# A hybrid of convolution and attention on one core: when pieces of other work are issued between the exponentials

## The chip, the cores and the metric

The kernel runs on one core of a Trainium2 chip. The metric is device time in microseconds (us) of one launch; the shown time is the median of three runs. A profile is one more execution, recorded by the hardware profiler, with its own time.

The engines that matter: TensorE (PE in the profile; PEld is its weight loads) multiplies, ScalarE (ACT) computes exp and tanh, VectorE (DVE) and GpSimd (POOL) do elementwise work, SyncE (SP) issues most DMAs. Each takes its instructions in the order of the program.

## The reference

The input x is 4 images of 64 x 64 pixels with 128 channels, float32. Two layers follow.

```python
# layer 0, per image of N = 4096 pixels
c1 = conv3x3(elu(x), W1) + b1
a, b = split(conv3x3(c1, W2) + b2)
c3 = a * sigmoid(b)
q, k, v = c3 @ Wq + bq, c3 @ Wk + bk, c3 @ Wv + bv      # 4, 4 and 16 wide
probs = softmax of q k^T / 4 over earlier pixels only
x = x + c3 + tile(probs @ v, 8) @ W3 + b3

# layer 1, on t = x as 4096 tokens
y = layernorm(t)
attn = 16 heads of width 8, full softmax(q k^T), no scale
h = y + attn @ wo
t = t + h + (silu(h @ w1) * (h @ w3)) @ w2              # 344 hidden
y = layernorm(t)
t = t + top-2 of 8 experts of y, weighted by the router's softmax
```

What costs most is layer 1's attention: 4 images x 16 heads x 4096 x 4096 exponentials.

## The kernel before

The function `fast_path` writes out every engine's order by hand: the class `InOrder` ties each instruction of an engine to the one before it. (A second function, `general_path`, serves inputs whose scores are out of range and isn't entered here.)

**Turns.** After a start in which the first image's first queries and keys are made, one loop at the end of `fast_path` runs the rest, a turn at a time. A turn is one step of attention: 128 keys of 4 heads against 512 queries. Four score matmuls write two of three PSUM buffers s, each 128 x 1024; two activations exp turn them into e in SBUF; later, value matmuls add e times the values into the one PSUM bank acc. The value matmuls of a step can be issued in quarters of 128 queries, and stay up to 8 quarters behind the scores (`undone`, `behind`, `must`). 32 steps make a segment: one group of 4 heads, one block of 512 queries. At its end VectorE copies acc to at, which is stored. There are 4 groups, 8 blocks and 4 images; the first image's segments are cut into parts, since its keys come one by one. 144 more steps are those of layer 0's attention (`first_step`).

**Pieces.** All other work is cut into pieces by generators: convolutions by a Winograd scheme (`convolutions`, `winograd`), layer 0's projections (`first_attention`), layer 1's operands (`second_operands`), and for each block of queries what follows attention (`last_part`: wo, the gated product, layer norm, router, experts). A piece is mostly a product into the one PSUM bank m, and a VectorE instruction that reads m. Its generator yields the TensorE time that it took and a word: "held" means that the bank holds half a product, "stop" that the next piece may come when there is room, "free" that the next turn shall begin with it.

**The planner.** The kernel is planned when it is built. `turn_at` is the planned start of the turn, 1.81 us apart. `dve_time` and `pool_time` keep clocks of VectorE and GpSimd, `dve_at` and `pool_at`; `bank_at` is when VectorE will have read m last. In each turn, after the scores, `left` is TensorE's planned room:

```python
    EXPS, SCORES, VALUES, PIECE, HEAD, AHEAD = 1.81, 0.54, 0.218, 0.446, 0.23, 0.2
...
        left = ahead + EXPS - SCORES - VALUES * must
        took, beside = None, False
        if not quiet[0] and fillers and fillers[0][3] and not waiting:
            took = insert()
...
        empty = bank_held[0] or bank_at[0] <= turn_at[0] + 0.3 or batches[b].second < NQ
```

A "free" piece comes first, whatever is left. Then the jobs of VectorE's tile (below), then up to two pieces, if the bank is empty, `credit` is above 0, and there is room (or `credit` is above 1.5). Then values take what is left, as long as more than 6 quarters are behind. Up to 0.2 us of unused room (`AHEAD`) is carried to the next turn. `credit` grows each turn by a rate that spreads the remaining pieces over the remaining steps, up to 3.0.

**VectorE's tile.** Of the 32 steps of a whole segment, step 20's exponentials are computed by VectorE instead of ScalarE, by a polynomial (the class `Beside`). The scores come in four units, one head each, through the bank m; each unit has a VectorE instruction that reads m into ey and eight more, queued in `beside_todo`. `beside_work(until)` issues these while VectorE's clock would finish them by `until`, which is the turn's planned start plus 2.9 us. When all four are made (`ready == NSLOT` and `done_at` no later than 0.4 us into the turn), two half products add them to acc. They read ey and write acc, not m. A job's `age` counts turns; its halves are due at 22 and 24. What isn't done at the segment's last values is forced then (`beside_rest`). There are 112 such tiles.

Of the kernel before, what the change touches and what calls it, by code (L numbers as in the profile page):

```python
# [21 lines left out]
NQ = N // QB  # L22
# [104 lines left out]
def fast_path(ctx: ExitStack, tc: tile.TileContext, a: dict, where: dict, out: bass.AP, verdict):  # L127
# [6 lines left out]
    nc = tc.nc  # L134
    x = a["x"]
    B = x.shape[0]
    pe, act, sp = (InOrder(tc, e) for e in (nc.tensor, nc.scalar, nc.sync))

    turn_at, dve_at, pool_at, bank_at = [0.0], [0.0], [0.0], [0.0]

    def pool_time(name, args):

        aps = [x for x in args if hasattr(x, "shape")]
        if aps and name != "dma_start":
            took = 0.65 + 1.25e-3 * int(np.prod(aps[0].shape[1:]))
            pool_at[0] = max(pool_at[0], turn_at[0] + 0.5) + took

    power_at, before, shift = [0.0], [None], [0.0]

    def dve_time(name, args):  # L150

        aps = [x for x in args if hasattr(x, "shape")]

        def reads(prefix):
            return any(x.name.startswith(prefix) for x in aps[1:])

        from_bank = reads("m_") or any(x.name == "m" for x in aps[1:])
        in_sbuf = not any(x.space == bass.MemoryType.PSUM for x in aps)
        took = max(int(np.prod(x.shape[1:])) for x in aps[:2]) / 960.0
        if in_sbuf and name in ("tensor_scalar", "tensor_copy"):  # L160
            took *= 0.5
        took += 0.075
        if any(x.name == before[0] for x in aps[1:]):
            took += 0.117
        before[0] = aps[0].name
        begins = 0.0
        if from_bank:
            begins = turn_at[0] + 1.1 + shift[0]
        elif reads("acc"):
            begins = turn_at[0] + 1.85  # L170
        elif reads("e_"):
            begins = turn_at[0] + 2.2
        elif reads("rs_") and name == "tensor_scalar":
            begins = power_at[0] + 1.3
        begins = max(dve_at[0], begins)
        if in_sbuf and begins < pool_at[0] - 0.2:
            took += 0.75
        dve_at[0] = begins + took
        if aps[0].name.startswith("ve_"):
            power_at[0] = dve_at[0]  # L180
        if from_bank:
            bank_at[0] = dve_at[0]

    dve, pool = InOrder(tc, nc.vector, dve_time), InOrder(tc, nc.gpsimd, pool_time)

    const = ctx.enter_context(tc.tile_pool(name="f_const", bufs=1))
    big = ctx.enter_context(tc.tile_pool(name="f_big", bufs=1))
# [254 lines left out]
    def winograd(u, cols, v, bias, used, final):  # L442

        late = []
        for q, j in enumerate(COLS):
            sd = chunk("sd")
            s, d = wk.tile([P, QB // 2], FP, tag="sums", bufs=1, name="sums"), sd[:, : QB // 2]
            for pair in ((1, 2), (0, 3)):
                if late:
                    late.pop(0)()  # L450
                ps = bank()
                part = [ps[:, : QB // 2], ps[:, QB // 2 :]]
                for m, i in zip(part, pair):
                    product(m, u[:, 4 * i + j, cols], v[q][:, i])
                    if i == pair[0]:
                        yield 0.46, "held"
                if pair[0] == 1:
                    if alone[0]:
                        act.activation(sd, ps, AF.Copy)
                    else:  # L460
                        dve.tensor_copy(sd, ps)
                    dve.tensor_tensor(s, d, sd[:, QB // 2 :], ALU.add)
                    dve.tensor_tensor(d, d, sd[:, QB // 2 :], ALU.subtract)
                else:
                    t = chunk("neg", "t2")
                    if q == 0:

                        dve.scalar_tensor_tensor(t[:, : QB // 2], part[0], bias, s, ALU.add, ALU.add)
                        dve.scalar_tensor_tensor(t[:, QB // 2 :], d, bias, part[1], ALU.add, ALU.subtract)
                    else:  # L470
                        dve.tensor_tensor(t[:, : QB // 2], part[0], s, ALU.add)
                        dve.tensor_tensor(t[:, QB // 2 :], d, part[1], ALU.subtract)
                    used(q)
                    if q == 0:
                        one = t
                    elif q == 1:
                        both, less = chunk("pos", "both"), chunk("pos", "less")
                        (dve if alone[0] else pool).tensor_tensor(both, one, t, ALU.add)
                        pool.tensor_tensor(less, one, t, ALU.subtract)
                    elif q == 2:  # L480
                        late += final(0, t, both, ALU.add)
                    else:
                        late += final(1, less, t, ALU.subtract)
                yield 0.46, "free" if q == 3 and pair[0] == 0 and late else "stop"
        while late:
            late.pop(0)()
            yield 0.0, "free" if late else "stop"
# [53 lines left out]
    def convolutions(b, st):  # L541
# [4 lines left out]
        def elu(n):  # L546
# [4 lines left out]
            for at in range(len(todo) + 2 if todo else 0):  # L551
# [10 lines left out]
                    act.activation(neg[a_], xs[a_], AF.Exp)  # L562
                if c_ is not None:
                    r, k = divmod(c_, 2)
                    ps = bank()
                    transposed(pos[c_], ps)
                    put = [(r, slice(1 + 8 * k, 9 + 8 * k), slice(0, 8))]
                    if k == 0 and r > 0:
                        put.append((r - 1, slice(17, 18), slice(0, 1)))
                    if k == 1 and r < 3:  # L570
                        put.append((r + 1, slice(0, 1), slice(7, 8)))
                    for band, to, of in put:
                        dve.tensor_scalar(
                            e_band[band % 2][:, to, 1 : IMG + 1], rows(ps)[:, of], -1.0, None, ALU.add
                        )
# [102 lines left out]
    def first_attention(b, st):  # L678
# [3 lines left out]
        for c in range(NQ):  # L682
# [10 lines left out]
            if c + 1 < NQ:  # L693
                xt = load_x(b, c + 1, "xt")

            ps = bank()
            yield from halves(ps, wq0, c3)
            u, qx0 = chunk("u"), chunk("qx0")
# [55 lines left out]
    def second_operands(b, st):  # L754
# [7 lines left out]
        cols = slice(c * QB, (c + 1) * QB)  # L762


        for pair in range(2):
            ps = bank()[:, : 2 * (C + 1)].rearrange("p (k c) -> p k c", k=2)
            for i in range(2):
                k = 2 * pair + i
                product(ps[:, i, :], at[:, k * P : (k + 1) * P], w3f)
            rs = small("rs0", [2])  # L770
            dve.tensor_scalar(rs, ps[:, :, C], 1e-35, None, ALU.add)
            dve.reciprocal(rs, rs)
            for i in range(2):
                tk = by_k(t)[:, 2 * pair + i, :]
                dve.scalar_tensor_tensor(tk, ps[:, i, :C], rs[:, i : i + 1], tk, ALU.mult, ALU.add)
            if pair == 1:
                st.read += 1
            yield 0.46, "free" if pair == 1 else "stop"
# [9 lines left out]
        yield from turned_over(h, yT, d["h"][c], "qx0", b == 0)  # L788
        def terms(i, w):

            ps = bank()
            yield from halves(ps, w, yT)
            u = chunk("u")
# [309 lines left out]
    def last_part(b, c):  # L1103
        d = scratch[b]
        while fetch(b, c):
            yield 0.0, "free"
        t, h, an = fetched.pop((b, c))
        ps = bank()
        tokens(ps, an, wo1, range(2))
        yield 0.46, "held"  # L1110
        tokens(ps, an, wo1, range(2, 4))
        dve.tensor_tensor(h, ps, h, ALU.add)
        yield 0.46, "stop"
        ps = bank()
        transposed(h, ps)
        hT = chunk("pos", "hT")
# [2 lines left out]
        yield 0.6, "stop"  # L1119
        gT = [chunk("u", "g0T"), chunk("qx0", "g1T"), chunk("w", "g2T")]  # L1120
        for n, (lo, size) in enumerate(FCH):
            ps = bank()
            yield from halves(ps, fw1[:, lo : lo + size], hT, size)
            h1, th = chunk("neg", "h1"), chunk("sd", "th")
# [5 lines left out]
            dve.scalar_tensor_tensor(h1[:size], ps[:size], 0.5, h1[:size], ALU.mult, ALU.mult)  # L1130
            dve.scalar_tensor_tensor(gT[n][:size], th[:size], 1.0, h1[:size], ALU.add, ALU.mult)
            yield 0.46, "stop"
        ps = bank()
        for m in range(4 * len(FCH)):
            k, n = divmod(m, len(FCH))
# [18 lines left out]
        if not alone[0]:  # L1154
            sp.dma_start(out=d["y"][c], in_=y)
        yield from turned_over(y, yT, d["y"][c], "neg", alone[0])
        ps = bank()
        few_by_token(ps[:, :P], rw, yT)
        scores = sm.tile([P, 4, SLOT], FP, tag="few", name="scores")
# [329 lines left out]
    credit, waiting = 0.0, False  # L1489


    EXPS, SCORES, VALUES, PIECE, HEAD, AHEAD = 1.81, 0.54, 0.218, 0.446, 0.23, 0.2
    ahead = 0.0
    while True:
        turn_at[0] += EXPS
# [22 lines left out]
            rate = (sum(part[1] for part in fillers) + later) / max(40, sum(steps_left) - 160)  # L1518
        credit = min(3.0, credit + rate)
        must = max(0, behind() - 8)  # L1520
        left = ahead + EXPS - SCORES - VALUES * must
        took, beside = None, False
        if not quiet[0] and fillers and fillers[0][3] and not waiting:
            took = insert()
# [2 lines left out]
        empty = bank_held[0] or bank_at[0] <= turn_at[0] + 0.3 or batches[b].second < NQ  # L1527
        for job in jobs:
            cost = HEAD if job.units < NSLOT else PIECE
            if job.can() and empty and (left >= cost or job.late()):  # L1530
                if not (quiet[0] or bank_held[0] or steps_in or waiting):
                    job.piece()
                    left -= cost
                    beside = True
# [17 lines left out]
        ahead = min(max(left, 0.0), AHEAD)  # L1552
        for job in jobs:
            job.step()
        beside_work(turn_at[0] + 2.9, any(job.age > 3 * job.units + 4 for job in jobs if job.halves < 2))
    finish(0)
    alone[0] = True
    run_alone([(r for part in fillers for r in part[0])], lambda: False)
# [717 lines left out]
```

## Time and profile before

| | us |
|---|---|
| median of 3 runs (2 others: 7976.11, 7983.8) | 7978.71 |
| the profiled execution | 7979.66 |
| its span, from the first to the last instruction | 7977.8 |
| TensorE busy (matmuls) | 7760.0 |
| ScalarE busy | 7661.9 |
| VectorE busy | 4798.3 |
| GpSimd busy | 671.5 |
| exponentials e, 8256 of them: busy | 7600.4 |

The clock granted to TensorE was 0.992 of full speed on average. All instructions bear the line of the helper that issues them (line 114), so groups are told apart by their tiles: s, e, acc, m and so on. A group's line gives its count, its busy time and the mean of one, and the engine's idle time just before it with what ended most of that time. A line of the view of waits says who waited for whom, the sum, how many times, and the longest. A matmul's recorded duration holds its passage through the array, while the next one runs already; so the sum of gaps between records is less than the time in which TensorE had nothing to issue. From 74.6 us to 7909.6 us after the start exponentials run; before it is the first image's start, after it the last block's `last_part`.

### The profile page before, as it was taken

What the parts mean: (1) busy time and instruction counts of PE and PEld (TensorE: products, weight loads), DVE (VectorE), ACT (ScalarE), POOL (GpSimd) and SP (SyncE); (2) the same over time, 40 slices, a digit from 0 to 9 for tenths busy, and PEclk for the clock granted to TensorE, in tenths of its full rate; (3) what the DMA queues carried; (4) which work ended last, traced back from release to release, by engine and by line L of the source; (5) the groups of instructions that cost most, each with busy time, mean ns of one, the idle gap of its engine ahead of it and who ended that gap; (6) DMA issues with size and microseconds to landing.
All of it is one profiled execution on the core that took longest, in us unless ns stands there. A gap on an engine that the chain in (4) does not pass through costs nothing.

```text
span 7977.8 us, 237947 instructions
## 1 busy us (share of the span) xinstructions
PE 7760.0 (97%) x103701; PEld 3280.2 (41%) x103701; DVE 4798.3 (60%) x9289; ACT 7661.9 (96%) x8459; POOL 671.5 (8%) x592
## 2 busy tenths in 40 slices
PE   7899999999999999999999999999999999999998
PEld 3333444444444444444444444444444333333334
DVE  4333556462666776666666776666666666666664
ACT  1899999999999999999999999999999999999996
POOL 1201211000022100000001210000000000000000
PEclk9999999999999999999999999999999999999998
DMA  2222011111110111111010011111111111111221
GB/s 71 70 68 69 23 60 33 60 41 53 35 34 15 50 39 50 38 31 43 25 41 29 19 43 43 51 42 34 33 29 52 50 49 53 50 54 50 70 73 38
DMA packets 334834, 360.96 MB, mean 45 GB/s; under 512 B 148211, under 2 KB 224467, under 8 KB 333779
## 3 DMA queue, kind: packets, MB, share of 16 engines
q1 hardware_dynamic: 329763, 343.87, 13.6%
q8 instruction: 814, 13.34, 0.7%
q10 hardware_dynamic: 4016, 1.77, 0.1%
q14 instruction: 241, 1.97, 0.1%
HBM read 209.50 MB, written 136.05 MB: 43 GB/s over the span
## 4 chain that ended last, share of the span: by engine, by line
PE 44%; issue 2%; DVE 2%; ACT 2%; DMA 0%; POOL 0%; SPq 0%; ACTq 0%; DVEq 0%; POOLq 0%
PE acc L114 22%; PE s L114 13%; PE m L114 9%; ACT e L114 1%; DVE ey L114 1%; DVE h L114 0%; DVE em L114 0%; DVE t L114 0%; DVE eg L114 0%; DVE by_e L114 0%; DMA blocks<-d_y 0%; SPq L114 0%; POOL rs L114 0%; DVE f_c_band L114 0%; DVE c L114 0%
## 5 line engine op out<-in xcount | busy, mean ns | idle before, releaser
L114 ACT ACTIVATE e<-s 128x1024 f32<-128x1024 f32 x8256 | 7600.4, 1113 | 111.2 <-PE s L114 106.6
L114 PE MATMUL acc<-e,vg 128*9 128x128 f32 (+3 forms) x61880 | 4278.8, 387 | 1.9 <-DVE at L114 1.8
L114 PE MATMUL s<-qx,f_kx 32*128 32x512 f32 (+1 forms) x16512 | 2556.8, 495 | 88.7 <-ACT e L114 56.4
L114 PEld LDWEIGHTS acc<-e,vg 128*9 128x9 f32 x61880 | 1562.0, 90 | 1777.6 <-issue 1209.5
L114 PEld LDWEIGHTS s<-qx,f_kx 32*128 32x128 f32 (+1 forms) x16512 | 1049.1, 182 | 2068.4 <-ACT e L114 1337.7
L114 DVE SCALAR_TENSOR_TENSOR ey<-ey,eg 128x512 f32<-128x512 f32 x1344 | 940.2, 700 | 31.9
L114 DVE COPY at<-acc 128x512 f32<-128x512 f32 x131 | 90.6, 691 | 597.9 <-PE acc L114 593.4
L114 PE MATMUL m<-v,f_wino 128*32 128x256 f32 x5376 | 420.2, 391 | 12.0 <-POOL v L114 7.3
L114 DVE TENSOR_SCALAR ey<-m 128x512 f32<-128x512 f32 x448 | 307.6, 687 | 89.8 <-PE m L114 80.0
L114 DVE SCALAR_TENSOR_TENSOR eg<-em,ey 128x512 f32<-128x512 f32 x448 | 316.7, 707 | 11.4
L114 DVE SCALAR_TENSOR_TENSOR ey<-ey,em 128x512 f32<-128x512 f32 x448 | 316.7, 707 | 9.5
L114 POOL TENSOR_TENSOR rs<-ve,f_minus_half 128x4 f32<-128x4 f32 x64 | 65.3, 1020 | 3027.4 <-DVE ve L114 2995.0
L114 DVE SCALAR_TENSOR_TENSOR ey<-eg 128x512 f32<-128x512 f32 x448 | 312.7, 698 | 0.0
L114 POOL TENSOR_TENSOR v<-r 128x1024 f32<-128x1024 f32 x112 | 219.1, 1962 | 975.4 <-PE m L114 975.0
L114 DVE COPY sd<-m 128x512 f32<-128x512 f32 x168 | 116.0, 690 | 301.5 <-PE m L114 301.1
L114 PE MATMUL m<-f_we,y2T 128*32 128x256 f32 x3968 | 291.9, 388 | 0.0
L114 DVE TENSOR_TENSOR by_e<-m,gates 128x512 f32<-128x512 f32 x248 | 170.3, 687 | 176.7 <-PE m L114 175.5
L114 PE MATMUL m<-hT,f_fw 128*32 128x256 f32 (+1 forms) x2728 | 233.0, 390 | 1.3 <-DVE hT L114 1.2
L114 POOL TENSOR_TENSOR t<-t,h 128x512 f32<-128x512 f32 x32 | 44.5, 1391 | 2240.6 <-DVE h L114 2240.6
L114 DVE TENSOR_TENSOR t<-m,t 128x512 f32<-128x512 f32 x61 | 42.2, 692 | 308.9 <-PE m L114 308.8
L114 DVE TENSOR_SCALAR em<-ey 128x512 f32<-128x512 f32 x448 | 200.4, 447 | 13.7
L114 DVE TENSOR_SCALAR em<-em 128x512 int32<-128x512 int32 x448 | 196.1, 438 | 10.0
(260 smaller groups left out, 4381.3 us busy)
## 6 DMA issues: line engine op xcount, KB each, us to landing
f_kx<-d_k SPq DMA_DIRECT2D x139, 512.0 KB
qx<-d_q SPq DMA_DIRECT2D x152, 256.0 KB
d_q<-two SPq DMA_DIRECT2D x64, 512.0 KB
d_a<-at SPq DMA_DIRECT2D x128, 256.0 KB
vg<-d_v SPq DMA_DIRECT2D x32, 576.0 KB
d_k<-two SPq DMA_DIRECT2D x32, 512.0 KB
d_v<-vc SPq DMA_DIRECT2D x32, 288.0 KB
xe<-in_x_dram SPq DMA_DIRECT2D x32, 256.0 KB
```

What stands on the lines that cost most here:

```text
L114: made = op(*args, **kw)
```

## The change

It has five parts, all in `fast_path`.

1. `ready_at` notes, for each tile that VectorE or GpSimd writes, the time on their build-time clocks at which it is made. `until_made(*tiles)` yields "free" without issuing anything as long as one of the tiles is made later than 0.4 us into the turn. It stands ahead of the products of v (Winograd), pos (transposes of elu), c3 (wq0), at (w3f), yT (wq1, wk1, router), an (wo1), h (transposes), hT (fw1) and the three gT (fw2). It does nothing in the start, or while the first image's operands aren't all made.
2. `act_time` counts activations that don't read PSUM, 0.16 us and 0.7 ns per element of a row (0.52 us for 512): tanh and the exponentials of xe. `left` of the next turn is larger by their sum.
3. `SCORES` is 0.55 for 0.54 and `PIECE` 0.456 for 0.446.
4. The half products of VectorE's tile are issued without the tests of the bank and of layer 0's steps, and don't keep other pieces out of the turn.
5. From a job's age of 19 on, with its halves not done, `beside_work` may issue VectorE's instructions up to 0.7 us further ahead per turn of age.

```diff
+    ready_at, act_more = {}, [0.0]
+
+    def act_time(name, args):
+
+        aps = [x for x in args if hasattr(x, "shape")]
+        if aps and name == "activation" and aps[1].space != bass.MemoryType.PSUM:
+            act_more[0] += 0.16 + 0.7e-3 * int(np.prod(aps[0].shape[1:]))
...
             pool_at[0] = max(pool_at[0], turn_at[0] + 0.5) + took
+            ready_at[aps[0].name] = pool_at[0]
...
         dve_at[0] = begins + took
+        ready_at[aps[0].name] = dve_at[0]
...
+    act = InOrder(tc, nc.scalar, act_time)
+
+    def until_made(*tiles):
+
+        while not alone[0] and batches[0].second == NQ and max(ready_at.get(x.name, 0.0) for x in tiles) > turn_at[0] + 0.4:
+            yield 0.0, "free"
...
+                yield from until_made(v[q])
                 ps = bank()
...
+            yield from until_made(c3)
             ps = bank()
             yield from halves(ps, wq0, c3)
...
-    EXPS, SCORES, VALUES, PIECE, HEAD, AHEAD = 1.81, 0.54, 0.218, 0.446, 0.23, 0.2
+    EXPS, SCORES, VALUES, PIECE, HEAD, AHEAD = 1.81, 0.55, 0.218, 0.456, 0.23, 0.2
...
-        left = ahead + EXPS - SCORES - VALUES * must
+        left = ahead + EXPS + act_more[0] - SCORES - VALUES * must
+        act_more[0] = 0.0
...
-            if job.can() and empty and (left >= cost or job.late()):
-                if not (quiet[0] or bank_held[0] or steps_in or waiting):
+            if job.can() and not (quiet[0] or waiting) and (left >= cost or job.late()):
+                if job.units == NSLOT:
+                    job.piece()
+                    left -= cost
+                elif empty and not (bank_held[0] or steps_in):
                     job.piece()
                     left -= cost
                     beside = True
...
-        beside_work(turn_at[0] + 2.9, any(job.age > 3 * job.units + 4 for job in jobs if job.halves < 2))
+        hurry = max([0.7 * (job.age - 18) for job in jobs if job.units == NSLOT and job.halves < 2] + [0.0])
+        beside_work(turn_at[0] + 2.9 + hurry, any(job.age > 3 * job.units + 4 for job in jobs if job.halves < 2))
```

The other eight calls of `until_made` stand in the same way ahead of their products.

More of the change, by code (lines that the diff above doesn't have):

```diff
@@ L136, in fast_path @@
     B = x.shape[0]
-    pe, act, sp = (InOrder(tc, e) for e in (nc.tensor, nc.scalar, nc.sync))
+    pe, sp = InOrder(tc, nc.tensor), InOrder(tc, nc.sync)
     turn_at, dve_at, pool_at, bank_at = [0.0], [0.0], [0.0], [0.0]
+    ready_at, act_more = {}, [0.0]
[3 more added lines that the diff above has]
+            act_more[0] += 0.16 + 0.7e-3 * int(np.prod(aps[0].shape[1:]))
     def pool_time(name, args):
@@ L564, in elu @@
                     r, k = divmod(c_, 2)
+                    yield from until_made(pos[c_])
                     ps = bank()
@@ L762, in second_operands @@
         cols = slice(c * QB, (c + 1) * QB)
+        yield from until_made(at)
         for pair in range(2):
@@ L789, in terms @@
         def terms(i, w):
+            yield from until_made(yT)
             ps = bank()
@@ L1107, in last_part @@
         t, h, an = fetched.pop((b, c))
+        yield from until_made(an)
         ps = bank()
@@ L1113, in last_part @@
         yield 0.46, "stop"
+        yield from until_made(h)
         ps = bank()
@@ L1121, in last_part @@
         for n, (lo, size) in enumerate(FCH):
+            yield from until_made(hT)
             ps = bank()
@@ L1132, in last_part @@
             yield 0.46, "stop"
+        yield from until_made(*gT)
         ps = bank()
@@ L1156, in last_part @@
         yield from turned_over(y, yT, d["y"][c], "neg", alone[0])
+        yield from until_made(yT)
         ps = bank()
```

## The prediction

> **What bounds the kernel now.** I read the page from the top, then the windows view of 400 to 7910 us (after the start, before the end), then who waited for whom in that stretch, then timelines of single waits.
>
> ```profile
> PE 7760.0 (97%) x103701; PEld 3280.2 (41%) x103701; DVE 4798.3 (60%) x9289; ACT 7661.9 (96%) x8459; POOL 671.5 (8%) x592
> PE   7899999999999999999999999999999999999998
> ACT  1899999999999999999999999999999999999996
> ...
> L114 ACT ACTIVATE e<-s 128x1024 f32<-128x1024 f32 x8256 | 7600.4, 1113 | 111.2 <-PE s L114 106.6 <-ACT e L114 0.6
> ...
> 400.00:7910.00 7510.00, 7401.23 (x101076) 3125.31 (x101072) 4613.33 (x8873) 7453.62 (x8225) 588.54 (x490) 1.00 0.14 44
> ```
>
> ScalarE and TensorE are both above 95% in every slice but the ends, so the one that sets the pace has to be found by waits.
>
> ```profile
> engine line waited for: us in total, times, longest us
> PEld s L114 <- ACT e L114: 1271.7, 2258, 1.7
> ...
> ACT e L114 <- PE s L114: 51.8, 45, 9.8
> ...
> PE s L114 <- ACT e L114: 54.2, 161, 1.0
> PE acc L114 <- DVE ey L114: 11.4, 10, 2.1
> PE s L114 <- DMA f_kx<-d_k: 10.2, 1, 10.2
> PE m L114 <- DVE f_e_band L114: 4.9, 3, 2.4
> PE m L114 <- DVE sd L114: 4.2, 6, 1.6
> PE m L114 <- DVE yT L114: 4.1, 6, 2.9
> PE m L114 <- DVE y2T L114: 2.4, 2, 1.5
> ```
>
> The reader is to see that the weight load of the scores s waits for ScalarE's e 2258 times, more than half of 4018 turns. That wait doesn't show as idle TensorE, because the matmul before it is still draining. **ScalarE is the bound.** Its exponentials start 904 ns apart when nothing is missing (4714 of the 8074 pairs of neighbours lie within 8 ns of that). I went through all their starts between 400 and 7905 us. 8037 of them at 0.904 us make 7265 us; the stretch has 235 us more. 83 us of it are tanh and exp of pieces (ScalarE takes 0.52 us more for a tanh), some 24 us are small change, and **128 us are turns in which ScalarE started 0.1 us after the scores ended, so TensorE was late**. These I sorted by what TensorE did in the turn. In 103 turns it stood still over 0.1 us for an input (63.3 us of ScalarE's time). In 1224 turns nothing was missing, and the turn was filled too full, by 53 ns each (65.1 us). TensorE itself waits 518 us inside the four score matmuls for the buffer, 0.13 us a turn. So it has room on the average, and what can be won is how its work is spread. That room can't be saved up: three score buffers let it be no further ahead, though the planner carries up to 0.2 us over.
>
> **The change, part by part, in ScalarE's time.**
>
> *Pieces put off (until_made).* Of the 63.3 us, waits for inputs at the places now guarded: yT 6.7, f_e_band or pos 6.2, y2T 2.2, c3 1.6, hT 1.5. To these comes at, which 22 of 24 products found made less than 0.1 us before (2.8 us in full turns). The clocks know only what stands before a tile on its engine. At 2668 us yT stood behind seven ey and em instructions, which they do know. At 2311 us VectorE itself waited 1.47 us for ScalarE's neg, and at 7805 us 2.5 us for blocks from a DMA, which they don't. So yT, c3, hT and at are in reach, 12.6 us; pos and y2T are not. Against it: a piece that comes back is taken at the turn's start without the tests of bank and room. The nearest row is the eb product, two pieces forced into one turn, late by 0.155 us 43 times; 60 pieces put off would cost 9 us so. The products themselves stay as many. I take **-8**, ends -13 and +9. While the first image's operands aren't done, until_made does nothing, so the 10.2 us for f_kx at 754 us stay.
>
> *VectorE's tile: halves without the bank test, and handed over early.* 448 units and 224 half products stay as they are. Waits for ey cost ScalarE 19.5 us in 10 places, and turns that hold a half and are too full 5.7 us. One such place:
>
> ```profile
> 1394.83 0.68 DVE L114 SCALAR_TENSOR_TENSOR ey<-eg 128x512 f32<-128x512 f32 x1
> 1395.54 2.14 DVE L114 SCALAR_TENSOR_TENSOR ey<-ey,eg 128x512 f32<-128x512 f32 x3
> 1395.76 0.11 PEld L114 LDWEIGHTS acc<-ey,vg 128*9 128x9 f32 x6 [0.24 <-issue]
> 1395.76 0.61 PE L114 MATMUL acc<-ey,vg 128*9 128x256 f32 x6
> 1397.72 0.69 DVE L114 SCALAR_TENSOR_TENSOR ey<-ey,em 128x512 f32<-128x512 f32 x1
> 1398.47 0.09 PEld L114 LDWEIGHTS acc<-ey,vg 128*9 128x9 f32 x1 [2.59 <-DVE ey L114]
> ```
>
> The half started at 1395.76 while the last ey ended at 1398.41: the build-time clock held the tile for made 2.7 us too soon, 13 turns before the segment's end. That error stays. What goes is the crowding at the end, where a half held back by the bank meets the last values. I take the 5.7 us and a quarter of the 19.5: **-10**, ends -25 and the rival below. Handing over earlier sets ey work ahead of the bank's readers on VectorE: at age 24 by 0.7 x 6 = 4.2 us, six instructions of 0.69 us. Behind these stand the copy out of m and, at a segment's end, at from acc; the next piece and the next segment's values wait for them. Now TensorE waits 4.2 us for sd and 2.1 us for ey out of m, 6.3 together. I take that two thirds of as much again come: **+4**, ends 0 and 60 (a wait of 0.54 us for each of the 112 tiles, half of the 2.9 - 1.81 = 1.09 us by which the work handed over reaches beyond a turn already).
>
> The Trainium skill speaks against this edit (PSUM — Partial Sum Buffer, section Engine vs sequencer instructions): VectorE's queue is a strict FIFO. By that rule alone, one reader of m caught behind each of the 112 tiles would cost up to 112 x 4.2 = 470 us, an estimate; the row at 2668 us shows one such wait, of 2.90 us. I stay with the small sum, since the planner puts no new piece on a bank whose reader its clock has late.
>
> *Lead counts tanh.* 93 tanh, 28 gate tanh and 26 exp of xe in the stretch take ScalarE 0.52 us each, 76 us in which TensorE now only waits (the tanh's followers: its weight loads waited 52.5 us for th). The turn after gets room for one piece more. Usable room grows from 518 - 76 = 442 to 518 us, by 17%; 17% of the 65.1 us are 11. I take **-10**, ends 0 and -30.
>
> *SCORES and PIECE 0.01 higher.* A turn with a piece is planned 0.02 us fuller than now, so one quarter of values (0.218) moves out in 0.02 / 0.218 = 9% of the turns. These are the fullest: 9% of 1224 are 110, at 0.08 us: **-9**, ends 0 and -25 (1224 x 0.02).
>
> The sum is -8 - 10 + 4 - 10 - 9 = -33. The profiled execution took 7979.66 us, its span 7977.8 and 1.9 around it; the median of the runs is 0.95 us lower. So 7978.71 - 33 = **7946 us**, and 7925 to 7962 if this is how it goes.
>
> **The rivals.**
>
> *The halves believe the clock too soon (slower).* In 12 of the 112 tiles the half stood in the stream before its last ey was done, in 12 more less than 1 us after, in 88 by 1 us or more, and much of that margin came from waiting for an empty bank. Without the test, halves come as soon as the clock says made. One wait cost 19.5 / 10 = 1.95 us. It decides from 33 / 1.95 = 17 more such tiles; with 30 the time is 7946 + 58 = 8004. For it: the 2.7 us error above, and VectorE's chains behind POOL and ScalarE, which the clock doesn't carry. Against: in the last batch, margins are 2 and 10 us.
>
> *Nothing (same).* The order of everything shifts with the first piece put off, and waits vanish in one place and come up in another; put-offs cover the cheap waits, while those from DMA and ScalarE stay. Time 7979, give or take 15. For it: no single row of the waits is over 0.3% of the time.
>
> *More than I count.* The full turns are the largest item. If three quarters of their 65.1 us go with the waits in reach (13) and the 25 for halves, 7979 - 49 - 13 - 25 + 4 is about 7896. For it: 1224 turns miss by only 53 ns, and the two constants are 20 ns. Against: the same values have to go somewhere.
>
> **How the numbers follow.** My forecast 0.47, more than I count 0.15, nothing 0.13, slower 0.25. About 0.2%, 16 us, can be told from no change; so faster 0.62, within 0.13, slower 0.25. The range goes from the third rival, 7892, to the slower one's price, 8004, which leaves out little more than its tail and the case that put-off pieces cost as well.
>
> **What would show it.** Right: waits of TensorE for yT, hT and c shrink while those for f_e_band and y2T stay; weight loads of s waiting for th fall well below 52.5 us; ScalarE's idle time before e, 51.8 us, falls by a third; halves stand earlier in the segment. Wrong: waits of acc for ey over 30 us, or of m for sd and ey over 15, mean the slower rival. Turns that are too full in the same number as before, with fewer waits, mean that the constants did nothing. Pieces left over for the end, after the last exponentials at 7910 us, would lengthen the tail, which I count at nothing because credit is kept through a put-off, up to 3 us.

## The result, and the profile after

The changed kernel takes **8018.68 us** (median of 5 runs, 8013.8 to 8021.95), against 7978.71 for the kernel before: 40 us slower, ratio 1.0049 with a 95% interval of 1.0034 to 1.0064. The prediction, 7946 and 7892 to 8004, missed the time and the sign.

The page of the kernel after, busy times and the exponentials' group:

```profile
PE 7794.0 (97%) x106565; PEld 3390.4 (42%) x106565; DVE 4804.1 (60%) x9289; ACT 7671.3 (96%) x8459; POOL 666.7 (8%) x592
...
L114 ACT ACTIVATE e<-s 128x1024 f32<-128x1024 f32 (+1 forms) x8256 | 7609.2, 1115 | 143.8 <-PE s L114 138.8
```

The work is the same: as many exponentials, as many VectorE instructions. TensorE has 2864 records more, since values are cut into quarters more often. What grew is ScalarE's idle time before e, from 111.2 to 143.8 us, and nearly all of it waits for TensorE's scores. The last exponential starts 41.9 us later than before. The profile splits the loss by who waited for whom, here from 400 us to the last exponential (us in total, times, longest):

```profile
ACT e L114 <- PE s L114: 84.0, 121, 9.8
...
PE s L114 <- ACT e L114: 61.8, 176, 0.4
PE acc L114 <- DVE ey L114: 14.7, 12, 3.3
PE s L114 <- DMA f_kx<-d_k: 9.9, 1, 9.9
PE m L114 <- DVE yT L114: 5.6, 6, 4.1
PE m L114 <- DVE f_e_band L114: 4.7, 3, 2.6
PE m L114 <- DVE ey L114: 4.0, 11, 1.0
```

ScalarE's waits rose from 45 to 121, from 51.8 to 84.0 us, while TensorE's own visible waits for VectorE rose by some 8 us only. So most of the loss isn't TensorE standing still, but turns that hold too much. I sorted the turns between 400 us and the last exponential in which TensorE was late (by over 20 ns) by what they hold. Each column has the number of turns and their lateness in us, in this order: before, after.

```
a half product, and a piece         0    0.0      89   31.5
a half product, no piece          124   26.9      69   38.2
no half: stood still over 0.1 us   90   42.1      75   46.6
no half: all others              1113   59.4    1070   58.4
sum                                     128.4           174.6
```

The half products of VectorE's tile make 42.8 of the 46.2 us. A new kind of turn appears, one that holds a half and a piece. The TensorE timeline of the kernel after shows two in a row (start us, duration, then what; a turn goes from one s to the next):

```profile
5610.65 0.51 PE L114 MATMUL s<-qx,f_kx 32*128 32x512 f32 x4
5611.09 0.62 PE L114 MATMUL acc<-ey,vg 128*9 128x256 f32 x8
5611.53 0.61 PE L114 MATMUL m<-f_we,y2T 128*32 128x256 f32 x8
5611.96 0.83 PE L114 MATMUL acc<-e,vg 128*9 128x384 f32 x8
5612.72 0.51 PE L114 MATMUL s<-qx,f_kx 32*128 32x512 f32 x4
5613.15 0.62 PE L114 MATMUL acc<-ey,vg 128*9 128x256 f32 x8
5613.59 0.61 PE L114 MATMUL m<-f_we,y2T 128*32 128x256 f32 x8
5614.02 1.04 PE L114 MATMUL acc<-e,vg 128*9 128x512 f32 x8
5614.99 0.50 PE L114 MATMUL s<-qx,f_kx 32*128 32x512 f32 x4
```

The turn from 5612.72 holds scores (0.43 us to the next start), a half (0.44), a piece (0.43) and a whole step of values (0.97): 2.27 us, where ScalarE needs 1.81. The turn before it, with three quarters of a step of values, took 2.07. ScalarE's timeline has the gap just behind them:

```profile
5615.59 1.94 ACT L114 ACTIVATE e<-s 128x1024 f32<-128x1024 f32 x2 [0.34 <-PE s L114]
```

### The profile page after: what moved, and what is told of

It is laid out like the page before. It is cut to its first block, busy times and chain, and to the rows that moved or that the text cites. A ratio compares the mean times of both kernels' runs of the same rounds, so it can differ in the third digit from the quotient of the medians.

```text
span 8019.3 us, 243681 instructions
## 1 busy us (share of the span) xinstructions
PE 7794.0 (97%) x106565; PEld 3390.4 (42%) x106565; DVE 4804.1 (60%) x9289; ACT 7671.3 (96%) x8459; POOL 666.7 (8%) x592
## 4 chain that ended last, share of the span: by engine, by line
PE 81%; issue 8%; DVE 5%; ACT 4%; DMA 1%; POOL 1%; SPq 0%; ACTq 0%; DVEq 0%; POOLq 0%
PE acc L114 40%; PE s L114 23%; PE m L114 18%; ACT e L114 3%; DVE ey L114 2%; DVE h L114 1%; DVE em L114 0%; DVE eg L114 0%; DVE t L114 0%; POOL rs L114 0%; DMA f_kx<-d_k 0%; DVE f_c_band L114 0%; DVE pos L114 0%; SPq L114 0%; POOL xt L114 0%
## 5 line engine op out<-in xcount | busy, mean ns | idle before, releaser
L114 ACT ACTIVATE e<-s 128x1024 f32<-128x1024 f32 (+1 forms) x8256 | 7609.2, 1115 | 143.8 <-PE s L114 138.8
L114 PEld LDWEIGHTS acc<-e,vg 128*9 128x9 f32 x64744 | 1641.2, 90 | 1779.8 <-issue 1184.3
L114 PEld LDWEIGHTS s<-qx,f_kx 32*128 32x128 f32 (+1 forms) x16512 | 1066.4, 182 | 1980.0 <-ACT e L114 1292.9
L114 DVE SCALAR_TENSOR_TENSOR h<-m,h 128x512 f32<-128x512 f32 (+1 forms) x93 | 64.2, 690 | 210.1 <-ACT th L114 188.1
```

The source lines that it names most:

```text
L114: made = op(*args, **kw)
```

## The experiments

Times are medians; each ratio is against the kernel before on the same chip, with a 95% interval. The kernel before took 7980 to 7981 us in these groups of runs. The interval of d_later_belief is wide because one of its 12 runs took 8084 us.

| run | parts of the change in it | us | ratio |
|---|---|---|---|
| a_old_halves | all but the new halves | 7987.21 | 1.0009 (1.0000 to 1.0018) |
| b_new_halves | new halves alone | 8000.34 | 1.0025 (1.0015 to 1.0036) |
| c_half_alone | all, no piece after a half | 7997.77 | 1.0022 (1.0013 to 1.0031) |
| d_later_belief | all, tile made 0.8 us later | 7997.00 | 1.0031 (1.0012 to 1.0049) |
| f_only_hurry | earlier hand-over alone | 8004.10 | 1.0028 (1.0018 to 1.0037) |
| g_only_constants | SCORES and PIECE alone | 7977.24 | 0.9998 (0.9989 to 1.0007) |
| h_only_tanh | tanh counted, alone | 7977.40 | 0.9994 (0.9985 to 1.0003) |
| i_only_put_off | until_made alone | 7984.85 | 1.0004 (0.9995 to 1.0013) |
| e_no_hurry | all but the hand-over | 8008.15 | 1.0035 (1.0021 to 1.0048) |
| l_no_tile_edits | put-offs, tanh, constants | 7967.38 | 0.9984 (0.9975 to 0.9993) |
| j_tanh_constants | tanh, constants | 7975.48 | 0.9995 (0.9986 to 1.0004) |
| m_alone_and_later | tanh, constants, repaired halves | 7982.73 | 1.0004 (0.9995 to 1.0013) |
| p_never_shared | all but the hand-over, halves apart from pieces | 7976.01 | 0.9994 (0.9985 to 1.0003) |
| s_half_hurry | as a_old_halves, half the hand-over | 7980.64 | 1.0002 (0.9992 to 1.0011) |

**First: the half products, or the rest?** a_old_halves puts the old tests back into the change; b_new_halves puts the new ones into the kernel before.

```diff
-            if job.can() and not (quiet[0] or waiting) and (left >= cost or job.late()):
-                if job.units == NSLOT:
-                    job.piece()
-                    left -= cost
-                elif empty and not (bank_held[0] or steps_in):
+            if job.can() and empty and (left >= cost or job.late()):
+                if not (quiet[0] or bank_held[0] or steps_in or waiting):
```

> The change with the old tests for the half products (bank empty, no half product open, no step of layer 0; no piece beside), all else kept. Theory H (the loss is the half products' new freedom: they share turns with pieces and start before ey is made): turns with a half that are late cost about 27 us of ScalarE's time again instead of 70, and the time is 7978.7 + 40 - 43 = 7975, give or take 10. Theory R (the loss comes from the other four parts, and falls on the halves only by chance): 8010 or more.

> The kernel before with the new tests for the half products alone. Theory H: 40 us slower, about 8019, with some 70 us of lateness in turns that hold a half. Theory R: within 10 us of before. A mixed case, where the new tests only hurt together with the raised room for tanh or the earlier hand-over, would lie between, about 7995.

a_old_halves came back to 7987.2, 31 us under the change; turns with a half cost 27.7 us, as before. b_new_halves lost 20 us alone, with 49.5 us in turns with a half. So the halves' new tests are the larger part, but theory H as stated fell short: it asked for 40 us from b and 7975 for a. Something else costs too.

c_half_alone adds `beside = True` after the half; d_later_belief changes when a tile counts as made.

```diff
                 if job.units == NSLOT:
                     job.piece()
                     left -= cost
+                    beside = True
```
```diff
-            return self.halves < 2 and self.ready == NSLOT and self.done_at <= turn_at[0] + 0.4
+            return self.halves < 2 and self.ready == NSLOT and self.done_at <= turn_at[0] - 0.4
```

> The change, but a turn with a half product takes no further piece, as before. Of the 43 us that turns with a half lost, 31.5 us stand in turns that hold a half and a piece. Theory H, sharing the turn: 8019 - 30 = 7989. If instead the start before ey is made does it (51 halves wait for ey, 31 us, against 16 and 17 us before): only about 8010. Theory R: 8015.

> The change, but VectorE's tile counts as made only 0.8 us later on its clock (done_at no later than 0.4 us ahead of the turn instead of 0.4 us into it). If the start before ey is made does it: waits of TensorE for ey fall from 31 to 15 us and the time by about 15 us, 8003. If sharing the turn with a piece does it: within 8 us of 8019. Theory R: no change.

Each took about 21 us off the change. In c, turns with a half and a piece fell from 31.5 to 1.1 us, while lone halves stayed at 37.0 (38.2 in the change). In d, halves that waited for an ey fell from 51 to 9, and that wait from 31 to 10 us, while turns with half and piece stayed at 26.2. Both mechanisms are real, then. By the turns' own lateness sharing is the larger one; by the time the two repairs are worth the same.

**Second: each other part alone.**

f_only_hurry has the two lines of `hurry` in the kernel before; g_only_constants the line of constants; h_only_tanh `act_time` and the sum in `left`; i_only_put_off `ready_at` and `until_made` with its ten calls.

```diff
+        hurry = max([0.7 * (job.age - 18) for job in jobs if job.units == NSLOT and job.halves < 2] + [0.0])
-        beside_work(turn_at[0] + 2.9, any(job.age > 3 * job.units + 4 for job in jobs if job.halves < 2))
+        beside_work(turn_at[0] + 2.9 + hurry, any(job.age > 3 * job.units + 4 for job in jobs if job.halves < 2))
```
```diff
-    EXPS, SCORES, VALUES, PIECE, HEAD, AHEAD = 1.81, 0.54, 0.218, 0.446, 0.23, 0.2
+    EXPS, SCORES, VALUES, PIECE, HEAD, AHEAD = 1.81, 0.55, 0.218, 0.456, 0.23, 0.2
```
```diff
-        left = ahead + EXPS - SCORES - VALUES * must
+        left = ahead + EXPS + act_more[0] - SCORES - VALUES * must
+        act_more[0] = 0.0
```
```diff
+            yield from until_made(yT)
             ps = bank()
             yield from halves(ps, w, yT)
```

> The kernel before with the earlier hand-over of VectorE's tile alone. Its own small theory, as in the prediction: +4, by more waits for readers of m (7 us now). The other: with the old tests halves wait for the bank anyway and the hand-over changes nothing, 0 give or take 5. If it makes up the 7 us that the change without its new halves lost: +15 or more.

> The kernel before with SCORES 0.55 and PIECE 0.456 alone. The prediction's step: turns that are too full (1224, 65 us) lose 9 us, time 7970. The other: the values that don't fit go to other turns and make these too full, so the count stays within 5% and the time within 5 us.

> The kernel before with tanh and exp of xe counted in the turn's room alone. The prediction's step: -10, and the weight loads of s wait clearly less than 52.5 us for th. The other: pieces that come earlier leave other turns emptier, which TensorE waits out; waits for th fall, yet the time stays within 5 us.

> The kernel before with until_made alone. The prediction's step: -8, with waits for yT, hT and c nearly gone, those for f_e_band, pos and y2T as before. The other: put-offs move the phase of all that follows, new waits come up elsewhere, and the time is within 5 us or up to 10 us longer.

The hand-over alone costs 23 us, the third case (+15 or more). Its profile doesn't show how. Of the 27 us between the two profiled executions, 9 lie after the last exponential (66.8 us in the kernel before, 75.6 in f_only_hurry): router and experts of the last block but one are left over for it, where the kernel before has only that block's eb product left. Pieces left for the end were the cost that the prediction counted at nothing. The rest are turns without a half in which TensorE stood still (some 22 us more by the sort above). Over the stretch from 400 us to 7900, TensorE's waits for VectorE, those of acc for ey left out, rise from 24.4 us in the kernel before to 42.1 us in f_only_hurry:

```profile
PE m L114 <- DVE y2T L114: 9.6, 6, 2.6
PE m L114 <- DVE pos L114: 6.9, 1, 6.9
PE m L114 <- DVE sd L114: 6.7, 8, 2.1
```

y2T stood at 2.4 us, sd at 4.2 and pos at none in the kernel before. The longest of them looks like the cause. VectorE's timeline of f_only_hurry, then GpSimd's, then TensorE's:

```profile
2313.89 6.33 DVE L114 SCALAR_TENSOR_TENSOR ey<-ey,eg 128x512 f32<-128x512 f32 x3
2320.14 2.14 DVE L114 TENSOR_SCALAR pos<-xe 128x512 f32<-128x512 f32 x1
2322.38 2.22 DVE L114 SCALAR_TENSOR_TENSOR pos<-neg,pos 128x512 f32<-128x512 f32 x1
```
```profile
2315.11 8.94 POOL L114 TENSOR_TENSOR v<-r 128x1024 f32<-128x1024 f32 x4
```
```profile
2324.66 1.11 PE L114 MATMUL m<-f_consts,pos 128*128 128x128 f32 x4 [6.92 <-DVE pos L114]
```

Three ey instructions stand in front of pos. Elsewhere they take 0.69 us each; here they take 6.33 us together, as GpSimd works on v at the same time, and pos is slow as well. TensorE stands 6.92 us for pos. But the hand-over didn't put them there. b_new_halves, which doesn't have it, shows the same chain and the same wait, on VectorE and on TensorE:

```profile
2316.49 6.34 DVE L114 SCALAR_TENSOR_TENSOR ey<-ey,eg 128x512 f32<-128x512 f32 x3
```
```profile
2327.27 1.11 PE L114 MATMUL m<-f_consts,pos 128*128 128x128 f32 x4 [6.92 <-DVE pos L114]
```

So does m_alone_and_later (6.91 us), which is described below. Nor does y2T wait behind ey. In the longest of its waits VectorE itself stood idle for a DMA:

```profile
7820.89 0.71 DVE L114 STREAM_TRANSPOSE y2T<-blocks 128x512 f32<-128x512 f32 x1 [3.60 <-DMA blocks<-d_y]
```

i_only_put_off, again without the hand-over, waits 8.4 us for y2T, and p_never_shared, also below, 8.9. So the two long rows come up with other shifts of the order as well. What is left of the kind that the prediction named, readers of m, is 2.5 us more each for sd and t. That this kernel is 23 us slower is shown; which waits the hand-over itself causes isn't.

Tanh and constants each gave 4 us, inside their intervals, so neither can be told from nothing. The count of tanh does what it says: weight loads of s waited 52.5 us for th in the kernel before, and no such row is left in the waits of h_only_tanh. The time hardly follows.

The put-offs alone gave nothing that can be told from the spread. The wait that I had named as in reach of the clock is still there, on TensorE's timeline of i_only_put_off:

```profile
2665.96 1.93 PE L114 MATMUL m<-yT,f_wq 128*32 128x256 f32 x16 [2.92 <-DVE yT L114]
```

It was 2.90 us. 22 of the 24 products of at still start less than 0.1 us after at is made, as before, and the waits for yT, hT and c are 4.2, 1.2 and 0.9 us against 4.1, 1.2 and 1.0. Waits for y2T rose from 2.4 to 8.4 us. The build-time clock took these tiles for made: in the plan that this kernel makes as it is built, until_made puts a piece off 24 times, each time for gT, and never for yT, c3, at or hT.

**Third: what the three parts do together, and the two tile edits apart.** e_no_hurry is the change without `hurry`; l_no_tile_edits also has the old tests for the halves; j_tanh_constants is h and g together; m_alone_and_later is j with the new halves, `beside = True` after each, and `done_at <= turn_at[0] - 0.4`.

```diff
-        beside_work(turn_at[0] + 2.9 + hurry, any(job.age > 3 * job.units + 4 for job in jobs if job.halves < 2))
+        beside_work(turn_at[0] + 2.9, any(job.age > 3 * job.units + 4 for job in jobs if job.halves < 2))
```

> The change without the earlier hand-over alone; new halves stay. If the hand-over costs here what it costs alone (23 us): 8019 - 23 = 7996. If new halves and hand-over are one cost, paid by either alone (20 and 23) and not by their sum (40): 8010 or more. The turns with a half should stay at some 60 us of lateness, the waits for y2T and pos fall.

> The change without both edits of VectorE's tile: put-offs, tanh and constants together on the kernel before. From the single parts (+4, -4, -4): 7977, give or take 7. The prediction's steps for these three would give 7980 - 27 = 7953.

> The kernel before with tanh counted and the two constants, no more. If the two gains are real and add up: 7980 - 8 = 7972 with 115 us of late turns. If they are the same few turns' luck: 7977 to 7981.

> The kernel before with tanh, constants and halves without the bank test, but with no piece in the turn of a half and with the tile counted as made 0.8 us later. If these two repairs take away all of what the new halves lose: late turns with a half under 20 us (27 before), waits of acc for ey under 8 us, and the time 7970 or below, under j_tanh_constants. If free halves are bad in themselves: above it by 10 us.

With both tile edits taken out, the change is **faster than both kernels: 7967.38 us**, ratio 0.9984 (0.9975 to 0.9993). Its late turns sum to 115.3 us, against 128.4. ScalarE's waits from 400 us to its last exponential:

```profile
ACT e L114 <- PE s L114: 45.6, 31, 9.3
```

The four corners on these three parts are then 7967 without tile edits, 7987 with the hand-over (+20), 8008 with the new halves (+41) and 8019 with both (+51), less than the sum of the two.

In e_no_hurry the halves' wait for ey is 12 us, less than the 17 of the kernel before, while turns with half and piece still lose 28.6 us. So the free halves cost by sharing the turn; the start before ey is made (31 us in the change) needs the hand-over as well. Turns that stood still without a half lost some 25 us more than in l_no_tile_edits, too, which nothing here explains. The hand-over adds 10 us on top of the new halves, where the two intervals meet. m_alone_and_later, 7 us above j, neither gained nor lost clearly; its halves cost 21.8 us in late turns, and its other waits rose, the 6.91 us for pos among them.

**Last: is it sharing alone, and does the depth count?** p_never_shared is e_no_hurry with a half barred from any turn in which a piece was taken first, and pieces barred after it. s_half_hurry is a_old_halves with 0.35 for 0.7.

```diff
                 if job.units == NSLOT:
-                    job.piece()
-                    left -= cost
+                    if not took:
+                        job.piece()
+                        left -= cost
+                        beside = True
```
```diff
-        hurry = max([0.7 * (job.age - 18) for job in jobs if job.units == NSLOT and job.halves < 2] + [0.0])
+        hurry = max([0.35 * (job.age - 18) for job in jobs if job.units == NSLOT and job.halves < 2] + [0.0])
```

> e_no_hurry (8008), with a half product never in one turn with a piece, neither after it nor after a piece that came first; it still doesn't ask for an empty bank. Turns with a half and a piece lost 28.6 us of ScalarE's time there, other waits rose by 25. If sharing the turn is all: those 28.6 us go and the time is 7980; if the other waits follow from it too: 7968, as l_no_tile_edits. If a half without the bank test is bad alone: 8000 or more.

> a_old_halves (7987, 20 above l_no_tile_edits at 7967) with the hand-over growing by 0.35 us a turn instead of 0.7. If the depth of VectorE's queue is what costs: 7972 to 7982, with TensorE's waits for VectorE's other work between 19 and 28 us. If any change of VectorE's order costs as much: 7987 again. If the 20 us are chance of the order: anywhere from 7960 to 7990.

p_never_shared came down from 8008 to 7976, so 32 of the 41 us went with the sharing: 27 in the turns themselves (turns with half and piece: 28.6 to 1.6 us), the rest in waits that fell with them. 9 us above l_no_tile_edits are left, where the runs of one kernel spread by some 5 us either way. s_half_hurry lies between: 7967, 7981 and 7987 at 0, 0.35 and 0.7 us a turn. The times fit a cost that follows the depth, but TensorE's waits for VectorE, acc's for ey left out, don't follow it: 19.0, 27.4 and 27.7 us. One order of instructions was built for each, so chance of the order isn't ruled out as a part of it.

## Why the prediction was wrong

**What failed: the step on VectorE's tile, "-10" and "+4".** It measured +41 for the halves and +20 for the hand-over, +51 together. The term for the halves counted the wrong thing, and the term for the hand-over was too small for a reason that stays open.

- *Halves.* I counted only what the old test cost, the crowding at a segment's end, and took for granted that the half goes where there is room. That the change also takes away `beside`, which kept pieces out of a half's turn, was in the diff and in my description, but not in the sum. A half and a piece of 0.456 us each, with 0.55 of scores and a step of values at 4 x 0.218, make 2.33 us planned, 0.52 over ScalarE's 1.81. The planner knows this and does it still: a late half ignores room, and so does a piece when credit is above 1.5. In the plan that the changed kernel makes as it is built, 105 turns take a half and a piece, and in 78 of them a piece comes in against room. No run changed that rule; that the sharing costs is shown by p_never_shared.
- *The hand-over.* "The planner puts no new piece on a bank whose reader its clock has late" was the reason for the small sum, +4. It measured +20 to +23, inside my own ends of 0 and 60. The strict FIFO of VectorE (the Trainium skill, PSUM — Partial Sum Buffer, section Engine vs sequencer instructions) was the warning. The trace of f_only_hurry agrees with it as far as order goes: pos ran after the three ey ahead of it. The estimate of 112 x 4.2 = 470 us was far too much. The row at 2668 us, which I had put beside it, isn't a reader of m at all: yT is an input of a product. Which waits make up the 20 to 23 us stays open, since the long ones stand in kernels without the hand-over as well.

**The slower rival** had the right place and the wrong mechanism. It said that halves without the test come before ey is made, at 1.95 us each, from 17 tiles on. In the changed kernel halves waited for ey in 51 places (16 before), with 366 ns in the median, not 1.95 us: 31 us against 17. That was the smaller part, and it goes when the hand-over goes (12 us in e_no_hurry). Of its signs, waits of m for sd and ey stayed low (5.5 us against 15), and acc's for ey are 14.7 us in TensorE's row and 32.4 in the weight loads', against 30. It took a turn that is too full for an input that is late.

**The put-offs, "-8".** Measured alone: 4 us slower, interval from 4 us faster to 10 us slower. "Which they do know" of the wait at 2668 us was wrong: the row is there unchanged, 2.92 us. From the order of instructions on VectorE I had argued that the clock must have it; the clock had already taken yT for made. The same goes for at. What until_made brings is not settled: together with tanh and constants it is 8 us better than these two without it (7967 against 7975), and intervals of +-7 us meet. In the whole change, the waits for yT, hT and c rose (5.6, 2.1 and 1.7 us), where the prediction's sign was that they shrink.

**Tanh, "-10", and the constants, "-9".** Too large: about 4 us each, and 5 for both together, all inside their intervals, so that even the sign isn't shown. The mechanism of the tanh was right, and its waits went. The full turns didn't follow: 65.1 us in 1224 turns of the kernel before, and the turns that hold a piece or nothing lose as much in the changed kernel (58.4 for 59.4 us). Spreading room better didn't empty the turns that are too full, and what fills them stays open. It isn't simply the pieces let in against room: as built, h_only_tanh does that 178 times where the kernel before does it 333 times, and its full turns without a half still lose some 57 us.

**What was right:** ScalarE's bound and its 0.904 us, that lost time is TensorE late to a turn, that pos and y2T aren't helped by until_made, that the 10 us of the keys' DMA stay (9.9 us after), and no cost at the end of the kernel: 66.6 us after the last exponential, 66.8 before (though f_only_hurry has one). The lower end of the range, 7892, is 4 us below the third rival's own sum; nothing rests on that.

## What to carry to other kernels

In a planned stream, a test that looks like one resource's (here: is the bank empty) can be what keeps two jobs out of one turn; before it goes, add up what a turn may hold without it, forced work included. Work handed early to an in-order engine cost 20 and 23 us in two pairs of kernels here, and the longest wait near it turned out to stand in kernels without it: before a wait is put down to a change, look for it in the runs that lack the change. And when a change bundles several small plans, the parts are worth measuring alone: here 13 us of gain lay under 51 us of loss.

## What the runs showed of the hardware

A VectorE instruction of 0.69 us (128 x 512, float32, from SBUF) took 1.70 to 2.30 us beside GpSimd's tensor_tensor over 128 x 1024, and three in a row took 6.33 us. The build-time clock adds 0.75 us for one, about half of what this place shows. Of the 2688 such polynomial instructions, 37 took over 1 us in the kernel before, 40 after, and every one of these overlaps a tensor_tensor of GpSimd by more than 0.1 us; of the 2625 and 2621 that don't, not one did.
